# A sign-delta layer and a LoRA layer on one core: engine orders and buffer places from a planner inside the kernel

## The chip, the core and the metric

The kernel runs on one core of a Trainium2 chip. A core has five engines, each with its own instruction stream: TensorE (PE, matmuls into the accumulators in PSUM), VectorE (DVE), ScalarE (ACT), GpSimd (POOL) and SyncE (SP). Transfers between HBM and the on-chip SBUF are issued by SP, ACT or POOL and carried by 16 DMA engines. The metric is the device time in microseconds; lower is better.

## What is computed

Two linear layers with residuals over x of 8 batches x 256 tokens x 1024 features, all in float32:

```python
# layer 0: each batch has its own 0/1 mask and its own coefficient
sign = 2 * mask - 1
x = x + (x @ W0.T + b0 + (x @ sign) * coeff[:, None, None])
# layer 1: one shared weight, and a LoRA adapter of rank 16 picked for each batch
A, Bm = lora_As[slot], lora_Bs[slot]
x = x + (x @ W1.T + b1 + (x @ A) @ Bm * 2.0)
```

In layer 0 the weight that meets a batch is W0 + coeff x sign + identity (the residual), another one for every batch. In layer 1 the weight W1 + identity is shared.

## The kernel before

Everything is transposed: features lie on partitions, tokens along the free axis. The work is done in two groups of four batches; a group passes layer 0 batch by batch, then layer 1 as one large product of the four batches.

**Layer 0.** A batch's mask comes in eight pieces of 512 KB (`load`, L179). ScalarE turns a piece into coeff x (2 x mask - 1) (L243), the DVE adds W0 with the identity in it (L251). Batch 0 runs piece by piece as W0 itself arrives (`first_batch`, L300, with its matmuls at L309), batches 1 and 2 as 64 matmuls of 128x128 weights by 256 tokens (`first_layer`, L269, L284). Batches 3 to 7 (`SEVEN`, class `Seven` at L335) are split into 2x2 blocks and done with seven block products where the plain way has eight (Winograd's form of Strassen's scheme): 7 x 16 matmuls of 128 tokens (L427). For that the DVE makes four sums of weight blocks (s1 to s4, L363, each as two operations of 128x1024) and four of tokens (t1 to t4, L380). Partial results stay in a PSUM bank: `X` gathers products, and is read after each step by ScalarE with the bias (L446) or by the DVE with an add (L453).

**Layer 1** (`second_layer`, L702) applies the scheme twice, 7 x 7 products of four matmuls each (L730). The outer seven have the names A11, A12, S1, S2, S4, S3, A22 and are done by `run` (L804) in that order; each has seven inner products a11, s1, s2, a12, s3, a22, s4. Banks are X, Y and Z: `begin` puts the first product into X, Z and Y are begun by their own first product, and `read` (L789) takes a bank out, with a ScalarE copy where the output is fresh (L791) and a DVE add where it is added to something (L793). X is read in the middle of its accumulation, so the product that adds to X next waits for that read. The adapters are the small matmuls `down` (L770) and `up` (L749).

**W1's leaves.** The 49 left operands (leaves) are sums of W1's blocks. `combine_weights` (L545) makes most of them while batches 1 and 2 run; `keep` (L537) stores those that are sums, or have the identity in them, to HBM through POOL, and both groups load all their leaves from HBM on SP (`load_leaves`, L711), seven buffers ahead. The remaining sums are made during batch 3 and in the first products of group 0's second layer; for S3, A11 and A21 are loaded again on POOL (`again`, L619).

**The order.** It is written by hand: generators are interleaved with the matmuls (`beside`, `step`, `ordered`), and `tc.issue_after` with named anchors holds an instruction behind another. Buffers come from rotating pools (L75 to L85).

Of the kernel before, what the change touches and what calls it, by code (L numbers as in the profile page):

```python
# [14 lines left out]
P = 128  # L15
OH = 512
CG = 2
OQ = 256
BY_HALF = 4
SEVEN = (3, 4, 5, 6, 7)  # L20
SCALING = 2.0


@with_exitstack
def kernel(
    ctx: ExitStack,
    tc: tile.TileContext,
    xT: bass.AP,
# [3 lines left out]

# [8 lines left out]

    nc = tc.nc
    B, NG, _, _, T = xT.shape
# [7 lines left out]
    S = 32  # L73

    const = ctx.enter_context(tc.tile_pool(name="const", bufs=1))  # L75
    wpool = ctx.enter_context(tc.tile_pool(name="weff", bufs=6))
    xpool = ctx.enter_context(tc.tile_pool(name="x", bufs=2))
    ypool = ctx.enter_context(tc.tile_pool(name="y", bufs=1))
    tpool = ctx.enter_context(tc.tile_pool(name="T", bufs=6))
    spool = ctx.enter_context(tc.tile_pool(name="t", bufs=8))  # L80
    lpool = ctx.enter_context(tc.tile_pool(name="leaf", bufs=7))
    qpool = ctx.enter_context(tc.tile_pool(name="q", bufs=10))
    bpool = ctx.enter_context(tc.tile_pool(name="lb", bufs=1))
    dram = ctx.enter_context(tc.tile_pool(name="dram", bufs=1, space=bass.MemoryType.DRAM))
    psum = ctx.enter_context(tc.tile_pool(name="ps", bufs=8, space=bass.MemoryType.PSUM))  # L85
# [3 lines left out]
    c_row = const.tile([1, B], F32, tag="c_row", name="c_row")  # L89
    nc.scalar.dma_start(c_row, coeff)  # L90
    one_row = const.tile([1, P], F32, tag="one_row", name="one_row")
    nc.vector.memset(one_row, 1.0)

    zeros = nc.const_aps.tensor(0.0, [P, T], F32)
    h_sb = const.tile([P, T], F32, tag="h", name="h_sb")
    idle_ps = psum.tile([P, T], F32, tag="ps", name="idle_ps")

    def idle(*columns: int):
        for n in columns:
            nc.tensor.matmul(  # L100
                idle_ps[:, :n], lhsT=zeros[:, :P], rhs=zeros[:, :n], start=True, stop=True
            )

    idle(T)
    c_ps = psum.tile([P, B], F32, tag="ps", name="c_ps")
    spread = nc.tensor.matmul(c_ps, lhsT=one_row, rhs=c_row, start=True, stop=True)
    with tc.issue_after(spread.ins):
        idle(T, T, T // 2)
    two_c = const.tile([P, B], F32, tag="two_c", name="two_c")
    nc.vector.tensor_scalar_mul(two_c, c_ps, 2.0)  # L110
    neg_c = const.tile([P, B], F32, tag="neg_c", name="neg_c")
    nc.vector.tensor_scalar_mul(neg_c, c_ps, -1.0)
    itok_sb = const.tile([1, B], I32, tag="itok", name="itok_sb")
    b0_sb = const.tile([P, NC], F32, tag="b0", name="b0_sb")
# [3 lines left out]
    lb_pad = const.tile([P, D], F32, tag="lb", name="lb_pad")  # L118
    ones = const.tile([1, T], F32, tag="ones", name="ones")
    nc.gpsimd.memset(ones, 1.0)  # L120

    def begin_adapters(late):


        nc.vector.tensor_copy(lb_pad[:, :1], late)
        nc.vector.tensor_copy(h_sb[:, :1], late)
        nc.gpsimd.memset(lb_pad, 0.0)
        nc.gpsimd.memset(h_sb, 0.0)
        for i in range(GB):
            one = slice(i * S + R, i * S + R + 1)  # L130
            nc.gpsimd.dma_start(lb_pad[one, :], b1)
            nc.gpsimd.dma_start(h_sb[one, :], ones)

    ident = const.tile([P, P], F32, tag="ident", name="ident")
    make_identity(nc, ident)


    x_sb, weff, raw, weff_at = {}, {}, {}, {}
    anchors = {}
    w0_sb = const.tile([P, NC, D], F32, tag="w0", name="w0_sb")  # L140
    by_half = [(h, g) for h in range(2) for g in range(NG)]
    by_seven = [(0, 0), (0, 1), (0, 2), (0, 3), (1, 2), (1, 0), (1, 3), (1, 1)]
    pieces = [(0, None, c) for c in range(NC)]
    pieces += [(b, h, g) for b in range(1, B) for h, g in (by_seven if b in SEVEN else by_half)]

    def behind(what: str):
        return tc.issue_after(anchors[what].ins) if what in anchors else nullcontext()

    def pair(name):
        return qpool.tile([P, 2, CG, OQ], F32, tag="q", name=name)  # L150

    def parts(k: int):

        every = slice(0, OH)
        if k == 0:
            quarters = [(slice(0, 1), slice(q * OQ, (q + 1) * OQ)) for q in range(2)]
            return quarters + [(slice(1, 2), every)]
        return [(slice(i, i + 1), every) for i in range(2)] if k < BY_HALF else [(slice(0, 2), every)]

    def part(a, i: int):  # L160

        flat = a.rearrange("p i f -> (p i f)")
        return flat.rearrange("(i p f) -> i p f", i=2, p=P)[i]

    def w0_of(k: int):
        b, h, g = pieces[k]
        if b == 0:
            return w0_sb[:, g, :].rearrange("p (h o) -> p h o", h=2)
        return w0_sb[:, g * CG : (g + 1) * CG, h * OH : (h + 1) * OH]


    W1_ORDER = [
        (2 * i + u, 2 * j + v)
        for i, j in ((0, 0), (0, 1), (1, 1), (1, 0))
        for u in range(2)
        for v in range(2)
    ]

    def load(k: int):  # L179

        b, h, g = pieces[k]

        if b in SEVEN and k % (2 * NG) >= 6 and b >= GB:
            pool, tag = qpool, "q"
        elif b in SEVEN and b % 2 and k % (2 * NG) < 6:
            pool, tag = tpool, "T"
        else:
            pool, tag = wpool, "w"  # L190
        weff[k] = pool.tile([P, CG, OH], F32, tag=tag, name=f"w_{k}")
        last = (k + 1) % (GB * 2 * NG) == 0
        pairs = [(weff[k].bitcast(I32), mask[b, g if b == 0 else h * NG + g])]
        if b == 0:
            pairs.append((w0_of(k), w0T[g]))
        x_pair = g // CG if b == 0 and g % CG == 0 else g if h == 0 else None
        if x_pair is not None:
            x = x_sb[b, x_pair] = xpool.tile([P, CG, T], F32, tag=f"x{x_pair}", name=f"x_{b}_{x_pair}")
        if k < BY_HALF:

            for i in range(2):
                for t, a in pairs:
                    nc.sync.dma_start(t[:, i], part(a, i))
                if k == 0 and i == 0:
                    nc.scalar.dma_start(x[:, 0], part(xT[0, 0], 0))
                elif k == 0:
                    nc.sync.dma_start(x[:, 1], part(xT[0, 0], 1))
                elif x_pair is not None and i == 0:
                    nc.sync.dma_start(x, xT[b, x_pair])
        else:  # L210
            for t, a in pairs:
                sent = nc.sync.dma_start(t, a)
            if last:
                anchors["masks"] = sent
            if x_pair is not None:
                nc.sync.dma_start(x, xT[b, x_pair])
        if k == NG:
            nc.sync.dma_start(b0_sb, b0)
        if k == 2 * NG:
            nc.sync.dma_start(itok_sb, itok)  # L220
        for n, (q, r) in enumerate(W1_ORDER):
            if k == 0 and r % 2 == 0:
                two = pair(f"w1_{q}_{r // 2}")
                raw[q, r], raw[q, r + 1] = two[:, 0], two[:, 1]
            if k == 2 * NG + 2 * n // 3:
                nc.sync.dma_start(raw[q, r], w1T[q, r])

    def build(k: int):

        b, h, g = pieces[k]  # L230
        if k == 2 * NG:

            for c in range(NC):
                d = w0_sb[:, c, c * P : (c + 1) * P]
                with tc.issue_after(weff_at[k - 1].ins):
                    nc.vector.tensor_add(d, d, ident)
        w = weff[k]
        m = w.bitcast(I32)
        for i, o in parts(k):


            with behind("bias"):
                nc.scalar.activation(  # L243
                    w[:, i, o],
                    m[:, i, o],
                    AF.Identity,
                    bias=neg_c[:, b : b + 1],
                    scale=two_c[:, b : b + 1],
                )
            with behind("adds"):  # L250
                weff_at[k] = nc.vector.tensor_add(w[:, i, o], w[:, i, o], w0_of(k)[:, i, o])  # L251
            anchors["weights"] = weff_at[k]

    loaded = 0

    def load_to(n: int):
        nonlocal loaded
        while loaded < min(n, n_pieces):
            load(loaded)
            loaded += 1  # L260

    LOADS_AHEAD = 4
    BUILDS_AHEAD = 2
    n_pieces = len(pieces)

    def bank(name):
        return psum.tile([P, 2, T], F32, tag="ps", name=name)

    def first_layer(b: int, h: int, y, beside):  # L269


# [896 lines left out]
```

## Time and profile before

| what | value |
|---|---|
| time, median of 3 runs | 405.8 us (405.55 to 407.65) |
| span of the profiled execution, first to last instruction | 404.0 us |
| TensorE clock granted | 1.000 |
| instructions in the span | 6794 |
| matmul records (two for each float32 matmul) | 2562 |
| DMA traffic | 99.56 MB, mean 246 GB/s |
| mask pieces: issues, time from issue to landing | 60 of 512 KB, 7.2 us |
| leaf stores on POOL, by kind | 44 of 256 KB, 3.7 to 6.8 us |
| leaf loads on SP | 98 of 256 KB, 2.8 to 3.2 us |

The span is what lies between the first and the last instruction in the profile; the page has no other time of that execution. In its rows of groups, the columns are source line, engine, operation, output and inputs with their shapes, count, busy us, mean ns of one, and the idle time of the engine in front of them with what ended it. PE's rows count records; PEld is the load of weights, which overlaps the matmuls.

### The profile page before, as it was taken

The numbers are of one execution on the slowest core, as the hardware profiler recorded it, in microseconds if no ns is written. First come the engines' busy times: TensorE is split into PE (matmuls) and PEld (weight loads), VectorE is DVE, ScalarE is ACT, GpSimd is POOL, SyncE is SP. The second block draws the span as 40 slices with busy tenths as digits, with TensorE's granted clock in tenths as the row PEclk, the third lists the DMA queues.
The fourth block names the chain that finished last, engine by engine and source line by source line (L and its number), as shares of the span: only waits on it lengthen the run. The fifth ranks groups of instructions, "written<-read, shape, count | busy, mean of one in ns | idle before, by whom it ended". The sixth has DMA issues, their size and how long they took to land.

```text
span 404.0 us, 6794 instructions
## 1 busy us (share of the span) xinstructions
PE 399.3 (99%) x2562; PEld 359.6 (89%) x2562; DVE 315.1 (78%) x451; ACT 128.8 (32%) x207; POOL 52.5 (13%) x103
## 2 busy tenths in 40 slices
PE   8999999999999999999999999999999999999997
PEld 6888888899978888888899999999998788888886
DVE  2447794999993779997989999998937346798694
ACT  4444624773113213004232927528222220100200
POOL 0000142105944220010130002100000000000000
PEclk9999999999999999999999999999999999999999
DMA  8999999990699799676998938831022337556663
GB/s 289 397 403 396 400 413 418 408 363 4 225 361 338 235 330 369 228 232 237 317 369 322 343 134 298 225 105 53 28 76 57 103 119 244 161 155 193 187 192 131
DMA packets 41700, 99.56 MB, mean 246 GB/s; under 512 B 5700, under 2 KB 6340, under 8 KB 41668
## 3 DMA queue, kind: packets, MB, share of 16 engines
q1 hardware_dynamic: 32978, 76.11, 54.6%
q0 software_dynamic: 6240, 18.90, 12.5%
q10 hardware_dynamic: 2450, 4.13, 2.8%
q8 instruction: 20, 0.33, 0.3%
q14 instruction: 12, 0.10, 0.1%
HBM read 79.19 MB, written 19.92 MB: 245 GB/s over the span
## 4 chain that ended last, share of the span: by engine, by line
PE 76%; DVE 12%; DMA 7%; issue 2%; SPq 2%; ACT 0%; DVEq 0%; ACTq 0%
PE X L730 23%; PE Z L730 11%; PE X L427 10%; PE ps L284 9%; PE ps L309 7%; PE Y L730 6%; PE Z L427 5%; DVE s L363 5%; DMA x<-xT 5%; DVE w L251 4%; PE G L749 2%; DVE t L380 2%; PE psh L770 2%; PE Y L427 2%; DMA l_A_s<-leaf_A_s 2%
## 5 line engine op out<-in xcount | busy, mean ns | idle before, releaser
L251 DVE TENSOR_TENSOR w<-w,w_sb 128x1024 f32<-128x1024 f32 (+2 forms) x69 | 77.6, 1142 | 28.5 <-ACT w L243 24.6
L243 ACT ACTIVATE w<-w,neg_c,two_c 128x1024 f32<-128x1024 int32 (+2 forms) x69 | 79.0, 1184 | 51.4 <-DMA w<-mask 47.2
L284 PE MATMUL ps<-x,w 128*128 128x256 f32 x256 | 55.4, 379 | 0.0
L284 PEld LDWEIGHTS ps<-x,w 128*128 128x128 f32 x256 | 48.6, 190 | 6.6
L446 ACT ACTIVATE y<-X,b_sb 128x128 f32<-128x128 f32 x60 | 17.1, 368 | 70.9 <-PE X L427 70.9
L427 PE MATMUL X<-t,s 128*128 128x128 f32 x288 | 34.1, 276 | 0.2 <-DVE s L363 0.2
L427 PEld LDWEIGHTS X<-t,s 128*128 128x128 f32 x288 | 33.0, 192 | 0.4 <-DVE s L363 0.4
L309 PE MATMUL ps<-x,w 128*128 128x256 f32 x128 | 28.5, 385 | 0.1
L309 PEld LDWEIGHTS ps<-x,w 128*128 128x128 f32 x128 | 24.3, 192 | 4.2 <-DVE w L251 0.9
L791 ACT COPY e<-X 128x512 f32<-128x512 f32 x14 | 8.2, 586 | 56.6 <-PE X L730 56.6
L793 DVE TENSOR_TENSOR c<-X,c 128x512 f32<-128x512 f32 x24 | 16.3, 686 | 11.2 <-PE X L730 11.2
L791 ACT COPY c<-G 128x512 f32<-128x512 f32 x16 | 8.2, 600 | 48.2 <-PE G L749 48.2
L427 PE MATMUL X<-t,w 128*128 128x128 f32 x192 | 22.5, 276 | 0.2 <-DVE y L453 0.2
L730 PE MATMUL X<-T_t,l_S_s 128*128 128x256 f32 x96 | 22.7, 379 | 0.0
L427 PEld LDWEIGHTS X<-t,w 128*128 128x128 f32 x192 | 21.9, 192 | 0.4 <-DVE y L453 0.4
L907 DVE TENSOR_TENSOR c<-c,e 128x512 f32<-128x512 f32 x32 | 21.6, 683 | 0.1
L363 DVE TENSOR_TENSOR s<-w,w 128x1024 f32<-128x1024 f32 x18 | 21.6, 1214 | 0.0
L730 PEld LDWEIGHTS X<-T_t,l_S_s 128*128 128x128 f32 x96 | 18.2, 190 | 2.5
L793 DVE TENSOR_TENSOR e<-Y,e 128x512 f32<-128x512 f32 x8 | 5.5, 690 | 17.3 <-PE Y L730 17.3
L427 PE MATMUL Z<-t,s 128*128 128x128 f32 x160 | 18.8, 275 | 0.0
L427 PE MATMUL Y<-x,w 128*128 128x128 f32 x160 | 18.7, 275 | 0.0
L427 PE MATMUL X<-x,w 128*128 128x128 f32 x160 | 18.7, 275 | 0.0
(147 smaller groups left out, 682.2 us busy)
## 6 DMA issues: line engine op xcount, KB each, us to landing
w<-mask SPq DMA_DIRECT2D x60, 512.0 KB, 7.2
l_S_s<-leaf_S_s SPq DMA_DIRECT2D x32, 256.0 KB, 3.2
x<-xT SPq DMA_DIRECT2D x31, 256.0 KB, 6.8
l_A_s<-leaf_A_s SPq DMA_DIRECT2D x24, 256.0 KB, 3.0
l_S_a<-leaf_S_a SPq DMA_DIRECT2D x24, 256.0 KB, 2.9
w<-w1T SPq DMA_DIRECT2D x16, 256.0 KB, 7.2
outT<-c POOLq DMA_DIRECT2D x15, 256.0 KB, 6.0
outT<-c ACTq DMA_DIRECT2D x15, 256.0 KB, 3.0
```

What stands on the lines that cost most here:

```text
L243: nc.scalar.activation(w[:, i, o], m[:, i, o], AF.Identity, bias=neg_c[:, b : b + 1], scale=two_c[:, b : b + 1],)
L251: weff_at[k] = nc.vector.tensor_add(w[:, i, o], w[:, i, o], w0_of(k)[:, i, o])
L284: nc.tensor.matmul(ps[j // 2][:, j % 2, :], lhsT=w[:, c, j * P : (j + 1) * P], rhs=x_sb[b, g][:, c, :],  start=first and j % 2 == 0, stop= ...
L309: nc.tensor.matmul(ps[ot // 2][:, ot % 2, :], lhsT=w[:, h, j * P : (j + 1) * P], rhs=x_sb[0, c // CG][:, c % CG, :], start=c == 0 and ot % ...
L363: anchors["weights"] = anchors["sums"] = op(s, self.w[x, a], self.w[y, a])
L380: nc.vector.tensor_sub(o, x, y)
L427: anchors["products"] = nc.tensor.matmul(ps[:, j, :], lhsT=w[:, c, j * P : (j + 1) * P], rhs=r, start=first and a == 0 and c == 0 and j == ...
L446: sent = nc.scalar.activation(self.out(i, v)[:, j, :], ps[:, j, :], AF.Identity, bias=b0_sb[:, ot : ot + 1])
L730: anchors["inner"] = nc.tensor.matmul(ps[:, j, :], lhsT=l[:, c, j * P : (j + 1) * P], rhs=r[:, c, :], start=first and c == 0 and j == 0, s ...
L791: anchors["copies"] = nc.scalar.copy(out, ps)
L793: own["reads"] = anchors["reads"] = nc.vector.tensor_add(out, ps, other)
L907: nc.vector.tensor_add(o, o, x)
```

## The change

The file is largely rewritten. What differs in the work:

- **Planner.** Each step becomes a `Task` with its engine, an estimated duration, what it reads and writes, and for some a due time. `Plan.order` keeps TensorE's steps in the order of the program, gives every other step a latest start (backward from the matmuls that need it), and then picks, engine by engine, the ready step that can start first, the tightest among equals. It gives each buffer a place as its first step is issued: 34 places of 128x1024, 16 of 128x512, 8 PSUM banks. The order comes out under `tc.manual_schedule()`; waits between engines are derived from reads and writes as before.
- **Batch 2** is done by sevens (`DENSE = (0, 1)`).
- **ScalarE copies PSUM bank to bank.** Y isn't begun by its own product: X's first product is copied into Y on ScalarE, and a12's product adds to it. Y then is read once, and the DVE's second add of the same output goes.
- **W1's sums** are made in group 0's second layer, where they are used from SBUF; group 0 loads no leaves. They are still stored for group 1. W1 comes as 8 transfers of 512 KB.
- **Smaller things.** xT comes as two transfers of 512 KB per batch from batch 1 on, and batch 0 has its own x0T. The identity is added to W0 before batch 0's own sums for six of the eight row blocks, whose results then need no x added: ScalarE reads them with the bias. Group 1's outputs go out on POOL, except the last pieces. The row of ones is `h_sb`, and the activation table's load stands ahead of the first x transfer on ScalarE.

```diff
-SEVEN = (3, 4, 5, 6, 7)
+DENSE = (0, 1)
+BIG, SMALL, BANKS = 34, 16, 8
...
+    def order(self, slots, idle):
+        for k in reversed(self.tasks):
+            late = [a.ls - self.WAKE - self.span(k) for a in k.after]
+            if k.engine == "PE":
+                late.append(k.due)
+            elif k.due is not None:
+                late.append(k.due - self.span(k))
+            k.ls = min(late, default=self.pe)
...
+                    t0 = min(s for s, _ in able)
+                    s, k = min(((s, k) for s, k in able if s <= t0 + 0.02), key=lambda c: (c[1].ls, c[1].n))
...
+        product("X", "a11", (0, 0), first=True)
+        weight_sum("s1", "add", "a21", "a22")
+        token_sum("t1", tokens(0, 1), tokens(0, 0))
+        product("Z", "s1", "t1", first=True)
+        copy(banks["Y"]((0,)), banks["X"]((0,)), OH)
+        biased(b, 1, 1, banks["Z"], 5)
...
+        product("X", "s2", "t2")
+        biased(b, 0, 1, banks["X"], 3)
+        product("Y", "a12", (1, 0))
+        biased(b, 0, 0, banks["Y"], 1)
...
+            s = small(f"{name}_{n}", CG, OQ)
+            x, z = (leaves[k] if isinstance(k, str) else k for k in (x, z))
+            leaves[n] = s((0,))
+            add(leaves[n], x, z, 512, op)
+            keep(n)
...
+    def leaves_of(name):
+        left[name] = left_first(name) if first else left_again(name)
...
-            read(out[0, 0], X, other[0, 0])
-            Z = bank(f"Z_{group}_{n}")
-            product(Z, leaf["s1"], r.t["t1"], first=True)
...
-            Y = bank(f"Y_{group}_{n}")
-            product(Y, leaf["a12"], r.b[1, 0], first=True)
-            read(out[0, 0], Y, out[0, 0])
...
+            Y = bank(f"Y_{group}_{n}", 2, T, seeded=True)
...
+            product(Z, leaf["s1"], t["t1"], start=True)
+            copy(Y((0,)), X((0,)), 512)
...
+            product(X, leaf["s2"], t["t2"])
+            read(out[0, 1], X, other[0, 1])
+            read(out[1, 1], Z, other[1, 1])
+            product(Y, leaf["a12"], rb(name, 1, 0))
+            read(out[0, 0], Y, other[0, 0])
```

## The prediction

> **What bounds the kernel now.** I read the busy rows first.
>
> ```profile
> span 404.0 us, 6794 instructions
> ...
> PE 399.3 (99%) x2562; PEld 359.6 (89%) x2562; DVE 315.1 (78%) x451; ACT 128.8 (32%) x207; POOL 52.5 (13%) x103
> ```
>
> TensorE has a matmul in flight for 399.3 of 404.0 us. That alone doesn't say that it issues at its full rate, so the next view is a table of two stretches: 36 to 76 us (batches 1 and 2, whole matmuls of 256 columns) and 260 to 300 us (batches by sevens, 128 columns). Columns: PE, weight load, DVE, ACT, POOL, clock, DMA share, GB/s.
>
> ```profile
> 36.00:76.00 40.00, 40.00 (x187) 35.23 (x186) 31.11 (x49) 20.06 (x22) 10.39 (x19) 1.00 1.03 409
> 260.00:300.00 40.00, 40.00 (x361) 40.00 (x360) 34.15 (x40) 17.02 (x36) 0.00 (x0) 1.00 0.20 64
> ```
>
> A float32 matmul leaves two records, so 36 to 76 holds 93 matmuls in 40 us, 0.43 us each; the clock is 1.00. Third, the waits of PE, and the largest one in the timeline:
>
> ```profile
> PE X L730 <- DVE c L793: 0.4, 1, 0.4
> PE X L427 <- DVE s L363: 0.2, 1, 0.2
> PE X L427 <- DVE y L453: 0.2, 1, 0.2
> ```
> ```profile
> 198.88 1.99 PE L730 MATMUL X<-T_t,l_A_s 128*128 128x256 f32 x8 [0.42 <-DVE c L793]
> ```
>
> Three waits in the whole run behind the start. Matmul ends are modelled, so I take starts: in these three places (98.1, 198.9 and 254.5 us) the next record starts 0.33, 0.58 and 0.33 us later than its cadence, and the one after it 0.10 us later: 1.5 us in all. The kernel is bound by TensorE's stream: 5.2 us ahead of the first real matmul, 396 us of stream, 2.9 us behind the last. A gain must shorten the stream or its two ends; a loss must be a new wait of PE.
>
> **Batch 2 by sevens.** It removes 64 matmuls of 256 columns and adds 112 of 128. The rows:
>
> ```profile
> L284 PE MATMUL ps<-x,w 128*128 128x256 f32 x256 | 55.4, 379 | 0.0
> ...
> L427 PEld LDWEIGHTS X<-t,s 128*128 128x128 f32 x288 | 33.0, 192 | 0.4 <-DVE s L363 0.4
> ```
> ```profile
> 261.93 3.57 PE Y L427 x32
> 265.50 3.57 PE X L427 x32
> 269.08 3.57 PE Z L427 x32
> ```
>
> L284 is two whole batches, 55.4 us: 27.7 for one. In the chain each of the seven products (32 records) lasts 3.57 us: 7 x 3.57 = 25.0. Gain 2.7 us, all on the path. A rule speaks against this. The Trainium skill, "Perfetto Trace Analysis", section "Identifying the Most-Contended Engine", says that matmul busy time is no measure of TensorE's headroom and that the busy share of weight loads is. By it the whole-batch stretch has room (35.23 of 40) and the sevens have none (40.00 of 40); with 192 ns for each of 224 loads, batch 2 would take 43 us and lose 15. But products of 3.57 us are 112 ns a record with those loads in them, so loads overlap each other, and I take 25.0.
>
> **Its other work.** On DVE batch 2 adds eight sums of 128x1024, four token sums and two reads. Over the kernel the built order has 132 tensor operations of 1024 where there were 116, 243 of 512 (252), 3 of 256 (44), and 2 fused bias operations (8). With the rows' 1217, 684, 415 and 476 ns: +19.5 -6.2 -17.0 -2.9 = -6.6 us, so DVE falls to about 308 us. This matters only where PE waits for it; the order shows where. Between batch 2's first product (the DVE must then be at its 36th instruction) and its fifth, 17.9 us of PE later (69th), lie 21 operations of 1024 and 13 of 512. Back to back these start 1.135 and 0.602 us apart in the trace: 31.7 us. DVE must enter the batch 14 us ahead. It can: the masks of batch 2 are the SP queue's rows 41 to 50, 20 MB from the start, 49 us at 406 GB/s (page: 396 to 413), while PE begins the batch at about 63 us. The DVE then is held at its 57th instruction until batch 1's bias reads end, about 64.5 us, and has 12 us of work to the 69th: 76.5, needed at 80. So 0, with 4 us of cover; were the masks 8 us late, half of it would show.
>
> **W1's sums.** They leave batches 1 and 2 (36 to 76 us, DVE 31 of 40) and go into group 0's second layer: 28 sums of 512, 8 of 1024. The second layer uses their results from SBUF, so its 49 loads of leaves on SP go, and the 8 reloads on POOL; the 44 stores of leaves on POOL stay, for group 1. W1 itself comes as 8 loads of 512 KB behind batch 3's masks on SP: the first waits for batch 1's last weights (about 63 us) and is needed past 95. From counts by size, HBM traffic falls by about 14 of 99.6 MB. Behind W1 on SP stand group 1's masks, not needed before 184 us. The DVE's load there: from the first sum behind batch 3 to the last read of the seventh product 96 operations of 512 and 18 of 1024: 57.8 + 20.4 = 78.2 us, beside 49 x 1.73 (the chain's 3.45 us for two products) + 7.5 (adapters: 3.58 + 2 x 1.94) = 92 us of PE. It fits as a sum; the tight places are PE's products into X, which wait for a DVE read of X one product earlier: 1.73 us of cover, against 0.20 (wake: Y's product starts at 393.97 or X's at 395.70, the DVE's read of the one before 0.20 later) + 0.69 + 0.06. That leaves 0.8 us, if no 1.135 us sum has just started. In the built order only one sum of 1024 (of S2, in run 0) ends just ahead of such a read, and it starts with the end of a product, 1.73 us before the read is released. Before, the same read stood behind an add (the wait at 198.9). I count 0.4 us for such waits, from 0 to 2.5.
>
> **ScalarE's bank-to-bank copies.** Twenty copies of X to Y (14 in the second layer, 6 by sevens) take the place of the DVE's add of Y, and PE's accumulation into X waits for each: a new wait. No row has a copy into PSUM; nearest is
>
> ```profile
> L791 ACT COPY e<-X 128x512 f32<-128x512 f32 x14 | 8.2, 586 | 56.6 <-PE X L730 56.6
> ```
>
> The cover is one product Z, 1.73 us, at the two places where X is begun directly before Z, and three or more products elsewhere. 0.20 + 0.59 + 0.17 = 0.96, so 0.8 us is left, even with ScalarE's own back-to-back 0.48 us ahead of it. A copy of 0.48 costs nothing and one of 1.2 costs nothing either; without cover it would be 0.9 x 20 = 18 us. I take 0. Queued behind each copy are conversions of masks, which run 20 us ahead.
>
> **The start.** This is the one loss that I can read. The activation table's load now stands ahead of the first x load on ScalarE:
>
> ```profile
> 1.42 0.37 ACTq L205 DMA_DIRECT2D x<-xT  x1
> 1.82 1.28 ACT L1020 ACT_TABLE_LOAD   x1 [1.82 <-PEq L1157]
> 3.11 0.20 ACT L1020 ACTIVATE warm<-one_row 1x1 f32<-1x1 f32 x1
> ```
>
> The load is issued 1.5 us later, at about 2.95. It landed 3.4 us after issue (4.82), hence now 6.35, where the first real matmul started at 5.23. Will it queue behind SP's six loads by then? As one line (0.65 us for each 256 KB) it would land at about 7.6. The Trainium skill, "DMA: Bandwidth & Descriptors", section "Queues, rings and completion order", says that each DMA engine takes turns between queue rows packet by packet; the trace agrees in that ACT's x packets run among SP's from 2.8 to 4.4 us. So 6.35. PE lost 0.6 us to waits just behind its first matmul (masks and sums), which a later start covers: 1.1 - 0.6 = 0.5, to 2.0 in the single line. I take 0.8, since eight small identity adds (0.2 us each) now stand in the first sums' chain.
>
> **The end.** The last pieces go out on SP and ACT as before; the store of (1,1) moves from ACT to POOL. POOL's stores land 3.4 us after issue when quiet, and it is issued 3 us ahead of the last piece's: 0.
>
> **The sum.** 404.0 - 2.7 (batch 2) - 1.5 (old waits, gone as the order around them is another) + 0.4 (new) + 0.8 (start) = 401.0. The page gives no time but the span; the median, 405.8, is 1.8 more, which stays: 402.8 us.
>
> **Rivals.** First, *the gain is there and is eaten*: x lands in single line (+1.2 on the main sum) and PE's waits stay as they were (+1.1): 405.1, no change. For it: the start has no cover. Against: packets do interleave. Chance 0.22. Second, *the leaf stores hold their places* (the slower side): t sums and leaves share 16 small places, and a place is free only when POOL's store of it has landed. If that is late, the DVE, in order, stands before a t sum, and behind it stand the reads of X that PE waits for. Stores landed in 3.4 to 8.5 us; in the built order a place is used again 10 us or more after its store's sum. It decides from about 12 us on; some twenty DVE operations of group 0's second layer wait for such a store, at 0.5 us each 10 in all, less the gain: 412.8 us. POOL's 60 stores in 92 us speak for it, 14 MB less traffic against. Chance 0.09. Third, *batch 2's lead isn't there*: masks or conversions late by 8 us, PE waits 4: 406.8, no change. Chance 0.05. Fourth, *no new wait and an early x*: 402.0. Chance 0.06. The main case: 0.58.
>
> **How the numbers follow.** A measurement of this kernel tells about 0.5% from no change, 2.0 us: faster is under 403.8, slower over 407.8. Main case and fourth rival are faster: 0.64; first and third are the same: 0.27; the second is slower: 0.09. The range takes in the main case with its bounds (start +0.5, no new waits: 402.1, less some of the 0.1 us restarts: 401.3) and the first rival with its own width: 401.3 to 406.2.
>
> **What would show it.** Right: PE's records at 216 and 112 ns, 224 records for batch 2, the first real matmul near 6.4 us, no wait of PE over 0.5 us, DVE near 308 us. Wrong: PE waiting for ACT's copy (cover gone), for DVE at X in group 0's second layer, DVE waiting for stores of leaves, or a first matmul past 7.5 us.

## The result and the profile after

| | before | after |
|---|---|---|
| time, median | 406.24 us (405.55 to 407.65, 4 runs) | 408.95 us (408.63 to 409.93, 4 runs) |
| span of the profiled execution | 404.0 us | 406.7 us |
| DMA traffic | 99.56 MB | 84.61 MB |

The ratio is 1.0067, 95% interval 1.0046 to 1.0087. The forecast was 402.8 us, 3.0 us less than the 405.8 known then; the change came out 2.7 us slower. The page of the profile, busy rows:

```profile
span 406.7 us, 6717 instructions
...
PE 396.4 (97%) x2654; PEld 360.9 (89%) x2654; DVE 314.8 (77%) x401; ACT 141.5 (35%) x241; POOL 52.1 (13%) x101
```

PE's busy time fell by 2.9 us, and the span grew by 2.7. So PE is idle longer, and the question is where. The waits of PE (total, times, longest):

```profile
PE bank L642 <- DVE big L300: 1.7, 2, 1.5
PE bank L334 <- PEq L1130: 0.9, 1, 0.9
```

The three waits of before are gone, and one pair in batch 2 (L642, products of the sevens) has come. That is 1.7 us, and doesn't explain the span. So I cut the run at two starts of records that every kernel here has: the first matmul of batch 1, and the last matmul of all.

| us | before | after |
|---|---|---|
| start: to batch 1's first matmul | 33.58 | 33.70 |
| stream: from there to the last matmul record | 367.21 | 365.20 |
| end: from there to the end of the span | 3.22 | 7.77 |

The stream did become 2.0 us shorter. The end is 4.55 us longer, and no engine is busy in it. What runs there are instructions of the engines' sequencers, which the busy rows don't count. They carry the line of the `with` block that the kernel stands in (L1163 before, L1136 after), and the view of that line shows them. Columns: engine, operation, count, duration in ns min/median/max, first and last start in us. Before, then after:

```profile
L1163 POOLq DRAIN  x3: 46/113/10412, 254.2 to 403.7; - x3
L1163 SPq DRAIN  x3: 7/7/7, 403.2 to 403.5; - x3
```
```profile
L1136 POOLq DRAIN  x3: 51/112/8311, 397.5 to 406.4; - x3
L1136 SPq DRAIN  x3: 7/7/7, 401.8 to 406.1; - x3
```

Each engine's list of instructions ends with DRAINs, instructions of its sequencer; the first one is the long one. GpSimd's begins with its last transfer and is long: 10.4 us before, from 254.2 us on, far inside the run. After, GpSimd issues the stores of group 1's outputs, the last one at 397.56; its DRAIN takes 397.54 to 405.85, while SP is through at 401.87. For four microseconds nothing else is left to do. (The other 0.55 us of the longer end: SP is through 2.98 us behind the last matmul record, before 2.43.)

The pair of waits, in the timeline (start, duration, in brackets the idle time ahead and what ended it):

```profile
78.46 2.36 DVE L300 TENSOR_TENSOR big<-big,big 128x1024 f32<-128x1024 f32 x2
80.73 1.22 DVE L300 TENSOR_TENSOR big<-big,w 128x1024 f32<-128x1024 f32 x1
...
80.87 2.05 PE L642 MATMUL bank<-big,big 128*128 128x128 f32 x16 [1.52 <-DVE big L300]
81.87 2.35 DVE L300 TENSOR_TENSOR big<-big,big 128x1024 f32<-128x1024 f32 x2
...
83.14 2.05 PE L642 MATMUL bank<-big,big 128*128 128x128 f32 x16 [0.22 <-DVE big L300]
```

PE waits for the two halves of batch 2's sum s4 (79.60 to 80.82 and 81.87 to 83.09); by starts of records it loses 1.78 and 0.48 us. Between the halves stands an add for batch 3's mask. The DVE has hardly any idle time from 57 us on, so it came late into the batch. ScalarE, which feeds it, shows since when:

```profile
46.12 1.24 ACT L387 ACTIVATE big<-big,neg_c,two_c 128x1024 f32<-128x1024 int32 x1 [0.45 <-DMA big<-mask]
48.26 1.24 ACT L387 ACTIVATE big<-big,neg_c,two_c 128x1024 f32<-128x1024 int32 x1 [0.90 <-DMA big<-mask]
52.18 1.24 ACT L387 ACTIVATE big<-big,neg_c,two_c 128x1024 f32<-128x1024 int32 x1 [2.68 <-DMA big<-mask]
```

The conversions wait for masks, which normally land 1.28 us apart (512 KB at 410 GB/s), here 2.0. Batch 2's last mask lands at 57.3 us. The transfers of 36 to 60 us say what shares the time with them:

```profile
DMA packets 2584, 9.02 MB, mean 376 GB/s; under 512 B 386, under 2 KB 386, under 8 KB 2582
...
q1 hardware_dynamic: 2326, 8.47, 96.2%
q0 software_dynamic: 256, 0.52, 6.2%
...
la<-lora_a POOLq DMA_DIRECT2D x4, 64.0 KB, 6.6
lb<-lora_b POOLq DMA_DIRECT2D x4, 64.0 KB, 6.5
```

GpSimd loads group 0's adapters from 40 to 53 us, as soon as the slot numbers have landed, though they are first used by the small matmuls at about 117 us. In the kernel before, these loads ran from 100.7 to 108.5 us: the planner moved them by 60 us, which the list of the changes doesn't have.

### The profile page after: what moved, and what is told of

Read it like the earlier page. It is cut to its first block, busy times and chain, and to the rows that moved or that the text cites. A ratio compares the mean times of both kernels' runs of the same rounds, so it can differ in the third digit from the quotient of the medians.

```text
span 406.7 us, 6717 instructions
## 1 busy us (share of the span) xinstructions
PE 396.4 (97%) x2654; PEld 360.9 (89%) x2654; DVE 314.8 (77%) x401; ACT 141.5 (35%) x241; POOL 52.1 (13%) x101
## 2 busy tenths in 40 slices
DMA packets 29779, 84.61 MB, mean 208 GB/s; under 512 B 4276, under 2 KB 4916, under 8 KB 29748
## 4 chain that ended last, share of the span: by engine, by line
PE 78%; DMA 12%; DVE 7%; ACT 1%; SPq 0%; issue 0%; DVEq 0%
PE bank L813 41%; PE bank L642 32%; DMA big<-mask 10%; DVE big L300 5%; PE bank L884 2%; PE bank L853 2%; DVE small L300 2%; DMA small<-x0T 2%; ACT big L387 1%; SPq L313 0%; PE bank L986 0%; ACT big L593 0%; DVEq L300 0%
## 5 line engine op out<-in xcount | busy, mean ns | idle before, releaser
L300 DVE TENSOR_TENSOR big<-big,big 128x1024 f32<-128x1024 f32 (+1 forms) x104 | 108.0, 1056 | 9.0 <-PE bank L642 3.6
L300 DVE TENSOR_TENSOR big<-bank,big 128x512 f32<-128x512 f32 (+2 forms) x99 | 65.8, 677 | 46.3 <-PE bank L813 33.4
L813 PE MATMUL bank<-small,small 128*128 128x256 f32 x384 | 89.0, 380 | 0.0
L642 PE MATMUL bank<-small,big 128*128 128x128 f32 x768 | 88.7, 275 | 0.0
L300 DVE TENSOR_TENSOR big<-big,w 128x1024 f32<-128x1024 f32 (+2 forms) x69 | 76.9, 1143 | 13.8 <-ACT big L387 9.0
L642 PEld LDWEIGHTS bank<-small,big 128*128 128x128 f32 x768 | 87.2, 192 | 0.0
L387 ACT ACTIVATE big<-big,neg_c,two_c 128x1024 f32<-128x1024 int32 (+2 forms) x69 | 78.3, 1179 | 21.2 <-DMA big<-mask 21.1
L813 PEld LDWEIGHTS bank<-small,small 128*128 128x128 f32 x384 | 72.9, 190 | 10.6 <-issue 0.8
L642 PE MATMUL bank<-big,big 128*128 128x128 f32 x576 | 67.6, 276 | 1.7 <-DVE big L300 1.7
L642 PEld LDWEIGHTS bank<-big,big 128*128 128x128 f32 x576 | 66.0, 192 | 2.2 <-DVE big L300 2.1
L472 PEld LDWEIGHTS bank<-small,big 128*128 128x128 f32 x128 | 24.9, 196 | 3.8 <-DVE big L300 0.3
L574 PEld LDWEIGHTS bank<-big,big 128*128 128x128 f32 x128 | 24.4, 190 | 3.3
```

The lines of the kernel that those rows point to most:

```text
L300: return dve(lambda: f(o.ap(), x.ap(), y.ap()), n, (x, y), (o,), due)
L387: lambda: nc.scalar.activation(o.ap(), x.ap(), AF.Identity, bias=neg_c.t[:, b : b + 1], scale=two_c.t[:, b : b + 1]),
L472: nc.tensor.matmul(dense[ot // 2].t[:, ot % 2, :], lhsT=w_b0[c].t[:, h, j * P : (j + 1) * P], rhs=x0[c // CG].t[:, c % CG, :], start=c == ...
L574: nc.tensor.matmul(ps[j // 2].t[:, j % 2, :], lhsT=w.t[:, c, j * P : (j + 1) * P], rhs=xs[g // 2].t[:, (g % 2) * CG + c, :], start=g == 0 ...
L642: nc.tensor.matmul(ps[:, j, :], lhsT=l[:, c, j * P : (j + 1) * P], rhs=m[:, 2 * a + c, :], start=first and a == 0 and c == 0 and j == 0, s ...
L813: nc.tensor.matmul(ps.t[:, j, :], lhsT=lt[:, c, j * P : (j + 1) * P], rhs=rt[:, c, :], start=start and c == 0 and j == 0, stop=False, skip ...
```

## The experiments

Theory: the run is slower because of two things that have nothing to do with each other, GpSimd's DRAIN (4 us at the end) and the adapters' transfers (2.3 us of waits in batch 2); everything else is a gain of about 4 us. Rivals: the end has another source; batch 2 waits because of the DVE's order (batch 3's adds ahead of s4), not of its lateness. The four kernels of the first round ran on one chip, with the kernel before at 406.08 us; so did the three of the second round, at 406.50. Between rounds, the ratios are what compares.

**The last two stores on ScalarE.** The other instructions keep their places.

```diff
-                    store(out[uv], *dest, *uv)
+                    store(out[uv], *dest, *uv, "ACT" if tail and n + 1 == len(OUTER) else None)
```

> The changed kernel with the two stores of outT that GpSimd issued last (394.99 and 397.56 us) on ScalarE instead; every other instruction keeps its place. Theory (the end is GpSimd's final DRAIN: 8.3 us long, begun with its last store at 397.54, while all other engines were through at 401.9): the drain now begins with the store at 392.3 and is over by about 400.6, ahead of the others; span 406.7 - 4.0 = 402.7 us, time about 405.0. Rival (the 5 us behind the last transfer have another source, the program's end or the landing of the stores): span stays at 406.7. Second rival (the drain is longer the more software transfers there were, and not tied to the last one): somewhere between.

Measured: 404.42 us (404.04 to 404.66), ratio to the kernel before 0.9953 (0.9937 to 0.9970), span 402.7. The last line's instructions:

```profile
L1136 POOLq DRAIN  x3: 51/113/8149, 392.7 to 402.4; - x3
L1136 SPq DRAIN  x3: 7/7/7, 401.8 to 402.1; - x3
```

The DRAIN is nearly as long as it was (8.1 us), but begins at 392.74 and is over at 400.89, ahead of SP. The end is 3.36 us, 4.4 less than in the changed kernel: 4.0 for the DRAIN, and 0.4 because SP too is through sooner (2.56 us behind the last matmul record, 2.98 there). Two stores on another queue turned a small loss into a small gain.

**One store on GpSimd in the kernel before.**

```diff
-            done((1, 1))
+            store(out[1, 1], *dest, 1, 1, queue=nc.gpsimd)
```

> The kernel before, with one single store of outT (256 KB, issued at 398.35 us on ScalarE) on GpSimd. Theory of the drain: it begins at about 398.4 and lasts 8.3 (as in the changed kernel) to 10.4 us (as it lasted in the kernel before, hidden at 254 us), so it ends at 406.7 to 408.8 where the other engines are through at 403.2: span 404.0 + 3.5 to 5.6 = 407.5 to 409.6. Rival (the changed kernel's end is long for another reason): one store changes nothing, 404.0.

Measured: 409.94 us (409.57 to 412.1), ratio 1.0098 (1.0074 to 1.0122), span 409.4, of which 1.3 us are a later start.

```profile
L1163 POOLq DRAIN  x3: 46/113/8428, 400.1 to 409.1; - x3
L1163 SPq DRAIN  x3: 7/7/7, 404.9 to 408.8; - x3
```

One store of 256 KB suffices: its DRAIN of 8.4 us ends at 408.57, 3.65 us behind SP's at 404.92. With the removal above this settles the end: it is the position of GpSimd's last transfer that counts, and one is enough. The second rival named with that removal, a DRAIN that grows with the number of GpSimd's transfers, stays untested: every kernel here has 92 to 95 of them.

**The slot numbers later.** The adapters wait for this load of 32 bytes.

```diff
-    dma("SP", itok_sb((0,)), itok, 32, due=50.0, ahead=20.0)
+    dma("SP", itok_sb((0,)), itok, 32, due=88.0, ahead=12.0)
```

> The changed kernel with the 32-byte load of the slot numbers moved on SP from among batch 2's masks to behind batch 3's masks; all else keeps its order. The adapters' loads on GpSimd wait for it, so they run at about 62 to 72 us and not at 40 to 53. Theory 1 (the adapters' small packets slow the masks: batch 2's fall from one in 1.28 us to one in 2.0 us and the last lands at 57.3): the masks land about 4 us sooner, the DVE is at batch 2's sum s4 in time, and the two waits of PE (1.78 and 0.48 us) go: span 404.4, time about 406.7. Theory 2 (the sum s4 is late because the DVE's order puts six of batch 3's mask adds ahead of it, which wait for batch 3's own masks): a part stays, span 405.5 to 406.7.

Measured: 407.27 us (406.59 to 408.01), ratio 1.0027 (1.0016 to 1.0038), span 404.6. PE's waits, and the transfers of 36 to 60 us:

```profile
PE bank L334 <- PEq L1130: 0.9, 1, 0.9
```
```profile
DMA packets 2689, 9.80 MB, mean 408 GB/s; under 512 B 300, under 2 KB 300, under 8 KB 2687
...
q1 hardware_dynamic: 2687, 9.78, 102.1%
```

Both waits are gone; the stream is 362.93 us, 2.27 less (the time, by the ratios, fell by 1.6). The queue of masks moved 9.78 MB in the same 24 us where it had moved 8.47: 1.31 MB more, 3.2 us at 408 GB/s, and batch 2's last mask landed at 54.1 us, 3.1 sooner. Of the 1.31 MB only 0.52 are the adapters' own bytes; the rest is rate lost while they ran (376 against 408 GB/s). It isn't that the adapters' packets are smaller, as the expectation has it: in the trace they have 4 KB, like those of the masks. But from 44 to 53 us a 4 KB packet of the masks took 198 to 247 ns (means of stretches of 2 to 3 us), and 163 ns before and after that. Why they slow down so stays open. Behind batch 3's masks the adapters disturb nobody.

**s4 in a place of its own.**

```diff
-        weight_sum("s4", "sub", "a12", "s2", into="a12")
+        weight_sum("s4", "sub", "a12", "s2", into=None if b == 2 else "a12")
```

> The changed kernel with batch 2's sum s4 written to two free places and not over a12, so that it need not wait for PE's product with a12; the planner then puts it 17 DVE instructions earlier, ahead of batch 3's mask adds. Theory 2 (order on the DVE: s4 may start only once PE has left a12, 3.5 us ahead of its own product, and then stands behind adds for batch 3): both waits go, 404.4. Theory 1 (the DVE as a whole is some 4 us late there): a wait of 1 to 2 us stays at that product or the next ones, 405.4 to 406.4.

Measured: 408.78 us (408.31 to 409.44), ratio 1.0064 (1.0047 to 1.0082), span 406.4. The stream is 363.79, 1.4 us less than the changed kernel's, but in the profile the start is 1.2 us later, in part by the slow first records (last section) and 0.3 us by a wait in batch 0, and the time shows next to nothing of the gain. Whether the timed runs had the later start too, no trace shows. In the stream:

```profile
83.97 0.69 DVE L300 TENSOR_TENSOR big<-bank,big 128x512 f32<-128x512 f32 x1
...
84.71 1.49 PE L642 MATMUL bank<-small,big 128*128 128x128 f32 x11 [0.60 <-DVE big L300]
```

The product with s4 now runs without a wait, but the next one waits 0.86 us for the DVE's read of X, which ended at 84.66. The order was a part of it, the lateness of the DVE the cause: taken from one instruction it shows at the next. The rival falls as the cause, since the earlier masks alone remove all of it, with the DVE's 401 instructions in the same order, by kind and shape, as in the changed kernel.

**Both mends together**, the slot numbers later and the two stores on ScalarE.

> The changed kernel with both mends: the slot numbers' load behind batch 3's masks, and GpSimd's last two stores of outT on ScalarE. They touch different ends of the run, so they should add: stream behind batch 0 shorter by 2.3 us, end shorter by 4.0: span 406.7 - 6.3 = 400.4 (the start varies by about 1 us from one execution to another), time 408.95 - 6.3 = 402.7, ratio to the kernel before 0.991. If they don't add (the shorter stream runs into a later wait), 404.5 as with the stores alone.

Measured: 402.43 us (402.15 to 402.82), ratio 0.9901 (0.9884 to 0.9918), span 400.9: they add, and this kernel beats both. Stream 362.93, end 3.36. The stretch of 62 to 88 us, batch 2, in the changed kernel and in the mended one (us, PE, PEld, DVE, ACT, POOL, clock, DMA share, GB/s):

```profile
62.00:88.00 26.00, 24.26 (x215) 23.88 (x214) 25.86 (x30) 13.18 (x22) 0.00 (x0) 1.00 0.56 212
```
```profile
62.00:88.00 26.00, 26.00 (x233) 25.97 (x232) 25.86 (x30) 14.63 (x28) 4.25 (x8) 1.00 0.60 208
```

The DVE does exactly as much in both (25.86 us): it has no reserve in this batch, and what decides is when its masks are there.

**Batch 2 whole again, in the mended kernel.**

```diff
-DENSE = (0, 1)
+DENSE = (0, 1, 2)
```

> The mended kernel with batch 2 as 64 whole matmuls of 256 columns again. If the sevens are worth what the forecast took from the rows (27.7 against 25.0 us) and bring no other cost once mended, this is 2.7 us slower than the mended kernel: about 405.4, span 403.1, ratio near 1.0. If the sevens' extra sums on the DVE eat part of it, it is less than 2.7 slower.

Measured: 404.91 us (404.29 to 405.28), ratio 0.9964 (0.9950 to 0.9978), span 403.2, stream 365.55. The sevens are worth 2.6 us of stream and 2.5 us of time; no part is eaten.

**Y begun by its own product, in the mended kernel** (the fourteen copies of the second layer undone).

```diff
-            Y = bank(f"Y_{group}_{n}", 2, T, seeded=True)
+            Y = bank(f"Y_{group}_{n}", 2, T)
...
-            copy(Y((0,)), X((0,)), 512)
+            read(out[0, 0], X, other[0, 0])
...
-            product(Y, leaf["a12"], rb(name, 1, 0))
-            read(out[0, 0], Y, other[0, 0])
+            product(Y, leaf["a12"], rb(name, 1, 0), start=True)
+            read(out[0, 0], Y, out[0, 0])
```

> The mended kernel with the fourteen bank-to-bank copies of the second layer undone: Y is begun by its own product, X is read into the output ahead of it (by ScalarE or, in ten runs, the DVE), and Y is added on the DVE: 14 more DVE operations of 512 (9.6 us of DVE in 180 us), 14 copies fewer on ScalarE. Theory of the forecast (the copies cost nothing and gain nothing for PE, as the DVE has room): same as the mended kernel, within 0.5 us. Rival (taking 14 reads from the DVE is what keeps the second layer of group 0, which now also makes W1's sums, free of waits): waits of PE for the DVE come back, 1 to 4 us.

Measured: 402.41 us (401.81 to 402.75), ratio 0.9897 (0.9880 to 0.9914), span 401.1, stream 362.93, the same to 0.01 us. The DVE's busy time is 322.4 where it was 314.3, and PE never waits for it. These fourteen copies neither cost nor gain.

## Why the forecast was wrong, step by step

Two steps failed: the end, put at 0, cost 4.55 us, and batch 2's cover on the DVE, put at 4 us, wasn't there and cost 2.3. The others were right or touched little.

- **Batch 2 by sevens, -2.7:** right; -2.6 by the pair of kernels above. The loss of 15 us, which the weight loads' 192 ns each would have made, did not come.
- **Old waits, -1.5:** right. From the stream before (367.21) to the mended one (362.93) it is 4.28 us; less 2.6 for the sevens leaves 1.7. This is a remainder; counted at the three places it was 1.5, and those waits are gone.
- **"So 0, with 4 us of cover" (batch 2's DVE work):** failed, 2.3 us. Its working put batch 2's masks at 49 us, 20 MB at the page's best rate. The last one landed at 57.3: 3.1 us are the adapters' transfers, which I had not placed in this stretch. About 2.8 us are the page's first slice, which has 293 GB/s and not 406, and about 1.9 us are 0.8 MB of later rows of the queue that had moved by then. The step named its own breaking point, masks 8 us late, and they were 8.3 us late. The DVE reached its 57th instruction at 68.45 us, having worked without a stop since 57.3, where I had it waiting until 64.5. Its work from there to the end of the 69th was sized rightly (12.4 us for 12), and so was the distance to the product with s4 (17.9 us; it is the sixth, not the fifth). What failed is when the masks are there. The third rival (masks late by 8 us, PE waits 4) is what happened, at a little over half its price; I had given it 0.05.
- **New waits in group 0's second layer, +0.4:** 0. W1's sums fit between the reads, and PE had no wait there beyond the restarts of 0.1 us that it had before. The second rival, leaf stores that hold their places, didn't come about: those stores landed within 2.6 to 4.5 us (medians by kind), and the DVE's waits have none for a store.
- **Bank-to-bank copies, 0:** right, though behind another 0.48 us of ScalarE the cover would have been 0.3 us and not 0.8. They take 570 ns, those into SBUF 594:

```profile
L304 ACT COPY big<-bank 128x512 f32<-128x512 f32 x32 | 17.6, 594 | 60.3 <-PE bank L813 30.6
L304 ACT COPY bank<-bank 128x512 f32<-128x512 f32 x20 | 11.4, 570 | 77.3 <-PE bank L813 53.6
```

- **The start, +0.8:** wrong, +0.1 in these two profiles. I had the x load wait for the table load ahead of it on ScalarE. The timeline after:

```profile
1.41 1.28 ACT L427 ACT_TABLE_LOAD   x1 [1.41 <-PEq L1130]
1.48 0.36 ACTq L313 DMA_DIRECT2D small<-x0T  x1
```

  ScalarE's sequencer issues the transfer 0.07 us into the table load. x landed at 4.49, where I had 6.35, and the first real matmul ran at 4.97 (before: 4.82 and 5.23). The +0.1 itself says little, as the start varies by more than that between executions (last section).
- **"it is issued 3 us ahead of the last piece's: 0" (the end):** this is the step that failed most, 4.55 us. I asked when the store lands (399.87 us, in good time), and not what the engine has to do behind it. None of the four rivals had it. Of the 4.55 us, 4.0 are GpSimd's DRAIN. A row that warns of it was in the profile of before, a DRAIN of 10.4 us in a place where nothing waited for it.

The sum with the measured terms: 404.0 - 2.6 - 1.7 + 2.3 + 0.1 + 4.55 = 406.65, for 406.7. (It closes in the stream because the -1.7 is a remainder.) DVE busy time was forecast near 308 and is 314.8. The durations did fall as counted, by 7.4 us in sum (343.1 to 335.7). But back-to-back operations overlap by 0.08 us, the busy row counts that time once, and with fewer of them the overlap fell by nearly as much, from 28.0 to 20.9 us. It touched no later step. Traffic fell by 15.0 MB, forecast 14.

## What to carry to other kernels

A transfer isn't over for the program when it has landed: look at what each queue's engine does behind its last one, and give GpSimd no transfer in the last 9 us or so (here 8.1 to 8.4 us of DRAIN behind a store and 0.8 us from there to the end). When a stage lives from masks or weights that just arrive, list everything that the queues carry in the same stretch, the small loads too, and place what isn't needed yet behind it; here one 32-byte load decided when half a megabyte of small loads ran. And cut the span at fixed records (start, stream, end) before explaining it: two losses and a gain of 4 us looked like one small loss.

## What the runs showed of the hardware that I hadn't expected

- GpSimd's DRAIN took 8.1 to 8.4 us behind stores of 256 KB in eight kernels here, and 10.4 us behind eight adapter loads. In the changed kernel it outlasts the landing of the last store (399.87 us) by 6.0 us, in the kernel before that of the last adapter load (260.72 us) by 3.9; what it does in that time no view shows.
- TensorE's first records of batch 0 come at half speed (0.43 us each) until a moment that isn't the same from one execution to another: the full pace (0.22 us) begins at 6.1 us before, at 7.0 after, at 9.0 with s4 in its own place, at 9.4 in the kernel before with one store moved, although that edit lies at 400 us. The granted clock in the profile's rows is 1.00 all the while. The start (to batch 1's first matmul) varies with it, from 33.6 to 34.9 us, though waits of batch 0 for the DVE have a part too (0.6 us in the kernel with two stores on ScalarE). The Trainium skill, "TensorE: Matmul & The Clock Gate", section "What's actually happening", says that the number of slow matmuls at the start differs between runs of one kernel; these traces agree. A difference of 1 us in one profile's span can be this alone.
- Eight loads of 64 KB on GpSimd cost the transfers beside them more than their bytes: 0.52 MB of adapters, and 0.78 MB less moved in all in those 24 us. GpSimd's queue alone doesn't do that: in the kernel before, 2.0 MB of leaf stores went through it in the same stretch, and the mean rate was 404 GB/s.
